# Transposes moved from TensorE to a DMA regrouping, and layer norms by sums, in a four-layer graph kernel

## The chip, the cores and the metric

The kernel runs on one core of one Trainium2 chip. The metric is the device time of one execution in microseconds (us), as a median of several executions. In what follows PE is TensorE, DVE is VectorE, ACT is ScalarE, POOL is GpSimd and SP is SyncE, the engine that issues the DMAs here.

## The reference, cut to what matters

Thirty-two graphs of 512 nodes with 256 channels pass through four attention layers, all over one mask `adj`. After each layer comes a residual addition and a layer norm without weights; layer 0 has two more layer norms inside it.

```python
x = _layernorm(x + _L0_gnn_ref(x, adj, w_qkv, ..., w1, b1, w2, b2))  # 8 heads, then a two-layer MLP
x = _layernorm(x + _L1_gnn_ref(x, W, a, adj))                        # additive scores, 1 head
x = _layernorm(x + _L2_gnn_ref(x, adj, W1, W2, W3))                  # product scores
x = _layernorm(x + _L3_gnn_ref(x, adj, W, a))                        # additive scores, 4 heads

def _layernorm(x, axis=-1, eps=1e-5):
    m = jnp.mean(x, axis=axis, keepdims=True)
    v = jnp.var(x, axis=axis, keepdims=True)
    return (x - m) / jnp.sqrt(v + eps)
```

Of the kernel before, what the change touches and what calls it, by code (L numbers as in the profile page):

```python
# [9 lines left out]
FP = mybir.dt.float32  # L10
# [20 lines left out]
AGE = 30.0  # L31
# [21 lines left out]
class Plan:  # L53
# [40 lines left out]
    def run(self, emit=True):  # L94
# [29 lines left out]
        while avail:  # L124
            cands = []
            for o in avail:
# [17 lines left out]
                for e, c in o.cost.items():  # L144
# [3 lines left out]
                    if best is None or key < best[0]:  # L148
# [5 lines left out]
                          key=lambda c: (not c[1].frees, c[1].graph * AGE - c[1].rank))  # L154
# [37 lines left out]
def kernel(  # L192
# [60 lines left out]
    def cbuf(shape, name, dt=FP):  # L253
# [37 lines left out]
        "D": [tc.dram_tile([H3, N], FP, name=f"r{i}") for i in range(6)],  # L291
        "PS": [psum.tile([P, N], FP, name=f"ps{i}") for i in range(8)],
# [5 lines left out]
    plan = Plan(slots, {"B": [14, 10, 10, 12], "S": [4] * 4, "T": [8] * 4, "D": [1] * 4, "PS": [0] * 4}, 5,  # L298
# [48 lines left out]
    def nodes(s):  # L347

        return lambda b: T2(b)[:, :, s * 2 * P:(s + 1) * 2 * P]

# [7 lines left out]

    def transposed(xs):

        xT = Buf("B")
        for s in range(2):
            ps = Buf("PS")

            def fn(e, s=s, ps=ps):
                for k in range(KC):
                    for j in range(2):
                        nc.tensor.transpose(two(ps)[:, k, j * P:(j + 1) * P],  # L368
                                            T4(xs)[:, 2 * s + j, k * P:(k + 1) * P], ident)
            op({"PE": 4 * TR}, fn, r=[xs[s]], w=[ps], pre=[xT])  # L370
            evac(ps, xT, s, nodes(s), two)
        return xT
# [12 lines left out]
    def project(xT, w, col, s, pre, row=None, part=None):  # L385

# [13 lines left out]
        op({"PE": 2 * F + (0.1 if row is None else 0.33)}, fn, r=[xT[part], w] + ([row] if row else []),  # L400
# [13 lines left out]
    def layernorm(y, dst, last=False, halves=(0, 1)):  # L414
        for s in halves:
            st, mv = Buf("T"), Buf("T")

            def stats(e, s=s, st=st, mv=mv):
                for j in range(2):
                    nc.vector.bn_stats(st.t[:, 6 * j:6 * j + 6], T4(y)[:, 2 * s + j, :])  # L420
                for j in range(2):
                    nc.vector.bn_aggr(mv.t[:, 2 * j:2 * j + 2], st.t[:, 6 * j:6 * j + 6])  # L422
            op({"DVE": 0.92}, stats, r=[y[s]], w=[st, mv])

            def scales(e, mv=mv):
                m = mv.t[:, :4].rearrange("p (c k) -> p k c", k=2)
                nc.gpsimd.tensor_scalar(mv.t[:, 4:6], m[:, 1, :], 1.0, EPS, ALU.mult, ALU.add)  # L427
                nc.gpsimd.tensor_tensor(mv.t[:, 6:8], mv.t[:, 4:6], mhalf[:, :2], ALU.pow)  # L428
                nc.gpsimd.tensor_scalar(mv.t[:, 8:10], m[:, 0, :], -1.0, 0.0, ALU.mult, ALU.add)
                nc.gpsimd.tensor_tensor(mv.t[:, 10:12], mv.t[:, 8:10], mv.t[:, 6:8], ALU.mult)  # L430
            op({"POOL": 1.6}, scales, r=[mv], w=[mv])
# [12 lines left out]
    def layer0(b, xs, xZ):  # L444
# [99 lines left out]
        u = Buf("B")  # L544
        for s in range(2):
            op(TH, lambda e, s=s: nc.vector.tensor_tensor(
                half(y, s), half(y, s), half(xs, s), ALU.add),
               r=[y[s], xs[s]], w=[y[s]])
        layernorm(y, u)
# [6 lines left out]
        hT, f, y2 = Buf("B"), Buf("B"), Buf("B")  # L556
        for k in range(KC):
            ps_h = project_t(w1_sb, 0, yT, k, hT)

            def relu(e, k=k, ps_h=ps_h):  # L560
                o, i, b = T2(hT)[:, k, :], ps_h.t, b1_sb.t[:, k:k + 1]
# [9 lines left out]
        for s in range(2):  # L571
            ps_f = project(hT, w2_sb, 0, s, f, c1p)
            op(TH, lambda e, s=s, ps_f=ps_f: nc.vector.tensor_tensor(
                half(f, s), ps_f.t, half(u, s), ALU.add), r=[ps_f, u[s]], w=[f[s]])
        layernorm(f, y2)
        for s in range(2):
# [3 lines left out]
            op(TH, lambda e, s=s: nc.vector.tensor_tensor(  # L580
                half(y2, s), half(y2, s), half(xs, s), ALU.add), r=[y2[s], xs[s]], w=[y2[s]])
        return y2

    def scored(xs, w, heads, val_shape, d1):
# [10 lines left out]

        xt = Buf("B")

        def xq():
            return xt.t[:, :NC * C].rearrange("p (q c b) -> p c q b", c=NC, b=32)
        for s in range(2):  # L600
            for c in (2 * s, 2 * s + 1):
                op({"DVE": cdve(256)}, lambda e, c=c: nc.vector.transpose(
                    xq()[:, c], T4(xs)[:, c, :].rearrange("p (q a) -> p q a", a=32)),
                    r=[xs[s]], w=[xt[s]])
# [51 lines left out]
    def layer1(xs):  # L656
# [7 lines left out]
        y, rinv = Buf("B"), Buf("T")  # L664
        for c in range(NC):
            ps = Buf("PS")

            def av(e, c=c, ps=ps):
# [7 lines left out]
            op({"DVE": 0.39}, lambda e, c=c, ps=ps: nc.vector.scalar_tensor_tensor(  # L676
                T4(y)[:, c, :], ps.t[:, :C], rinv.t[:, c:c + 1], T4(xs)[:, c, :],
                ALU.mult, ALU.add), r=[ps, rinv[c], xs[c // 2]], w=[y[c // 2]])
        track(NC * H0, NC, rinv, NC * H0)
        return y  # L680

    def layer2(xs):
        xT = transposed(xs)
        gT, v = Buf("B"), Buf("B")
        for k in range(KC):
            evac(project_t(w12_sb, 0, xT, k, gT), gT, k, lambda b, k=k: T2(b)[:, k, :])
# [3 lines left out]
        for s in range(2):  # L690
            evac(project(xT, w3_sb, 0, s, v, part=s), v, s, lambda b, s=s: vv()[:, 2 * s:2 * s + 2, :C], two)
        op({"DVE": 0.08}, lambda e: nc.vector.memset(vv()[:, :, C:C + 1], 1.0), r=[xT], w=[v])
        y = Buf("B")
        for s in range(2):
            a, low_, pT = Buf("B"), Buf("T"), Buf("B")
            for j in range(2):
# [46 lines left out]
            op(TH, lambda e, s=s: nc.vector.tensor_tensor(  # L743
                half(y, s), half(y, s), half(xs, s), ALU.add),
               r=[y[s], xs[s]], w=[y[s]])
        return y

    def layer3(xs):
# [45 lines left out]
        ex, y = Buf("B"), Buf("B")  # L794
# [665 lines left out]
```

## The kernel before: the parts that the change and the argument touch

The kernel doesn't issue its instructions graph by graph. It first describes each graph as operations, each with an estimated cost on each engine that could take it, and a list scheduler (the "plan") then simulates the engines and emits everything in one fixed order. On the chip each engine runs its own part of this order, strictly in order. So the scheduler's costs never run on the chip, but they decide what stands in front of what.

```python
AGE = 30.0
LAT = {"PE": 0.3, "DVE": 0.15, "ACT": 0.2, "POOL": 0.25, "SP": 4.0}   # from an operation's end to its result
# ... in Plan.run: an operation that can start first is placed; older graphs have priority
            s, o, e = min((c for c in cands if c[0] <= tmin + 0.05),
                          key=lambda c: (not c[1].frees, c[1].graph * AGE - c[1].rank))
# ...
            for n in o.succ:
                n.npred -= 1
                n.ready = max(n.ready, f + LAT[e])
# ... five graphs in flight:
    plan = Plan(slots, {"B": [14, 10, 10, 12], ...}, 5, {"DVE": 1.0})
    DMA = 0.53                                                        # planned cost of one DMA issue
```

Transposes for layer 0's MLP and for layer 2 are made on PE, eight of 128x128 for each, and copied out of PSUM by `evac`. A new graph comes in by `block`, four DMAs in runs of 128 bytes that leave each 32x32 block in a form that DVE can transpose:

```python
    def transposed(xs):
        xT = Buf("B")
        for s in range(2):
            ps = Buf("PS")
            def fn(e, s=s, ps=ps):
                for k in range(KC):
                    for j in range(2):
                        nc.tensor.transpose(two(ps)[:, k, j * P:(j + 1) * P],
                                            T4(xs)[:, 2 * s + j, k * P:(k + 1) * P], ident)
            op({"PE": 4 * TR}, fn, r=[xs[s]], w=[ps], pre=[xT])
            evac(ps, xT, s, nodes(s), two)
        return xT

    def layernorm(y, dst, last=False, halves=(0, 1)):
        for s in halves:
            # ... DVE: two bn_stats, two bn_aggr
            # ... POOL: four small instructions make scale and shift
            # ... ACT or DVE: two normalizations of 128x256

        def block(e, b=b, xZ=xZ):                       # the load of a new graph
            v = x[b].rearrange("(j b) (k i a) -> i b k j a", b=32, k=KC, i=4)
            for i in range(4):
                nc.sync.dma_start(
                    T2(xZ)[32 * i:32 * i + 32].rearrange("p k (j a) -> p k j a", a=32), v[i])
        op({"SP": 4 * DMA}, block, w=[xZ])
```

## Time and profile before

| | before |
|---|---|
| time, three executions | 3023.44 us (3019.7 to 3026.94) |
| span of the profiled execution | 3020.5 us |
| PE, DVE, ACT, POOL busy | 98%, 87%, 56%, 29% |
| PE lost in 2700 to 3021, by busy time | 53.9 us |

PE is busy in every microsecond from 200 to 2700. But a matmul that waits for its turn can count as busy, so I also kept a second account of PE, used below for every run. From the timeline of PE I took each group of equal instructions, from its start to the start of the next group, and subtracted the number of instructions times the shortest slot that such an instruction shows in a row (0.43 us for 512 columns of f32, about 0.216 for 256 columns, 0.109 for a transpose, and so on). What is left is lost. A loss of over 0.5 us at one place I call a gap; the rest, 0.1 to 0.3 at a time, are switches between matmuls of different shape. "Mid-run" is from 200 us to some 290 us before the end.

### The profile page before, as it was taken

The page shows a single profiled execution, that of the slowest core. Times are in us where ns is not written, and L with a number is a line of the kernel's source. Part 1 is how long each engine was busy: PE and PEld are TensorE (multiplying, and loading weights), DVE is VectorE, ACT ScalarE, POOL GpSimd, SP SyncE. Part 2 cuts the span into 40 slices and gives each one's busy share as a digit, 9 for nine tenths or more (in the row PEclk, how much of TensorE's full clock was granted, in tenths as well). Part 3 has the DMA queues.
Part 4 walks back from the last instruction along what each step waited for, and adds up shares of the span by engine and source line. Part 5 has one row for each costly group of instructions (what it writes and reads, how often), then busy time and mean ns, then how long its engine had stood idle before and what let it go on. Part 6 is the DMA issues. An engine that isn't in the chain of part 4 may idle for free.

```text
span 3020.5 us, 49063 instructions
## 1 busy us (share of the span) xinstructions
PE 2947.4 (98%) x17898; PEld 1633.3 (54%) x17898; DVE 2635.2 (87%) x5277; ACT 1688.5 (56%) x3475; POOL 866.8 (29%) x1809
## 2 busy tenths in 40 slices
PE   8999999999999999999999999999999999999885
PEld 3465555555555555555555555555555555555452
DVE  7988899988899988899988899988899988889754
ACT  5546655665655665555665555665555665655432
POOL 0223322322322322322322322322322322322221
PEclk9999999999999999999999999999999999999997
DMA  7000110111110110110110110110110111110000
GB/s 139 12 19 22 39 39 19 40 39 22 39 39 19 39 40 22 39 39 18 40 40 22 39 39 19 40 39 22 39 39 19 40 39 24 37 32 19 32 25 29
DMA packets 194746, 102.67 MB, mean 34 GB/s; under 512 B 143937, under 2 KB 181313, under 8 KB 194497
## 3 DMA queue, kind: packets, MB, share of 16 engines
q1 hardware_dynamic: 193648, 97.63, 12.9%
q8 instruction: 142, 2.33, 0.3%
q10 hardware_dynamic: 848, 1.84, 0.2%
q14 instruction: 108, 0.88, 0.1%
HBM read 82.31 MB, written 17.12 MB: 33 GB/s over the span
## 4 chain that ended last, share of the span: by engine, by line
PE 92%; DVE 4%; issue 1%; DMA 1%; ACT 1%; POOL 1%; SPq 1%; DVEq 0%; ACTq 0%; POOLq 0%
PE ps L380 15%; PE ps L397 11%; PE ps L467 9%; PE ps L475 8%; PE ps L611 8%; PE ps L765 7%; PE ps L730 7%; PE ps L703 7%; PE ps L670 7%; PE ps L771 4%; PE ps L368 2%; PE ps L722 2%; PE ps L536 1%; PE ps L701 1%; PE ps L802 1%
## 5 line engine op out<-in xcount | busy, mean ns | idle before, releaser
L340 ACT ACTIVATE b<-ps 128x512 f32<-128x512 f32 x772 | 434.9, 602 | 497.2 <-PE ps L380 186.9
L486 DVE TENSOR_TENSOR b<-b,maskT 128x1024 f32<-128x1024 f32 x512 | 594.5, 1212 | 25.1 <-ACT b L480 25.1
L480 ACT ACTIVATE b<-ps 128x512 f32<-128x512 f32 x1024 | 528.4, 604 | 116.7 <-PE ps L475 116.7
L439 ACT ACTIVATE b<-b,t 128x256 f32<-128x256 f32 x768 | 425.6, 597 | 255.9 <-POOL t L430 244.3
L427 POOL TENSOR_SCALAR t<-t 128x2 f32<-128x2 f32 x384 | 135.2, 352 | 845.0 <-DVE t L422 777.8
L757 DVE SCALAR_TENSOR_TENSOR b<-b,s,maskT 128x512 f32<-128x512 f32 x512 | 358.7, 740 | 8.0 <-DMA b<-r 7.7
L428 POOL TENSOR_TENSOR t<-t,mhalf 128x2 f32<-128x2 f32 x384 | 340.0, 885 | 32.0
L475 PE MATMUL ps<-b,b 32*128 32x512 f32 x2048 | 300.4, 640 | 0.0
L498 DVE TENSOR_TENSOR b<-b,b 128x1024 f32<-128x1024 f32 x256 | 297.4, 1210 | 0.0
L420 DVE BATCH_NORM_STATS2 t<-b 128x6 f32<-128x256 f32 x768 | 284.4, 412 | 7.8 <-DVE b L580 0.5
L408 POOL TENSOR_TENSOR acc<-acc,s 128x32 f32<-128x32 f32 (+2 forms) x96 | 77.3, 806 | 637.8 <-DVE s L525 378.1
L467 PE MATMUL ps<-b,b 128*32 128x512 f32 x2048 | 250.9, 598 | 2.6 <-DVE b L486 2.3
L765 PE MATMUL ps<-b,b 128*64 128x512 f32 x1024 | 239.3, 606 | 13.1 <-DVE b L757 13.1
L380 PE MATMUL ps<-b,wqkv_sb 128*128 128x512 f32 x512 | 248.1, 609 | 0.0
L397 PE MATMUL ps<-w_sb,b 128*128 128x256 f32 x1024 | 245.6, 388 | 1.4 <-ACT b L340 1.4
L703 PE MATMUL ps<-b,b 128*128 128x512 f32 x512 | 240.6, 592 | 0.0
L380 PE MATMUL ps<-b,w_sb 128*128 128x512 f32 x512 | 235.5, 603 | 2.5 <-ACT b L340 2.5
L670 PE MATMUL ps<-b,b 128*128 128x257 f32 x1024 | 230.8, 383 | 2.5 <-issue 2.5
L730 PE MATMUL ps<-b,b 128*128 128x257 f32 x1024 | 228.5, 380 | 0.4 <-ACT b L340 0.4
L670 PEld LDWEIGHTS ps<-b,b 128*128 128x128 f32 x1024 | 195.8, 192 | 45.4 <-issue 10.6
L397 PEld LDWEIGHTS ps<-w_sb,b 128*128 128x128 f32 x1024 | 190.0, 191 | 53.8 <-issue 30.0
L408 POOL TENSOR_TENSOR acc<-acc,t 128x2 f32<-128x2 f32 (+2 forms) x128 | 37.9, 308 | 598.7 <-DVE t L789 325.7
(124 smaller groups left out, 4129.8 us busy)
## 6 DMA issues: line engine op xcount, KB each, us to landing
b<-r SPq DMA_DIRECT2D x64, 512.0 KB
b<-in_x_dram SPq DMA_DIRECT2D x128, 128.0 KB
b<-in_x_dram SPq DMA_DIRECT2D x32, 512.0 KB
out_dram<-b SPq DMA_DIRECT2D x64, 256.0 KB
b<-r SPq DMA_DIRECT2D x32, 256.0 KB
r<-s SPq DMA_DIRECT2D x128, 0.5 KB
r<-s SPq DMA_DIRECT2D x128, 2.0 KB
b<-in_adj_dram ACTq DMA_DIRECT2D x4, 256.0 KB
```

The source lines that it names most:

```text
L340: nc.scalar.activation(dst, src, AF.Copy)
L380: nc.tensor.matmul(ps.t, w.t[:, i, col + k * P:col + (k + 1) * P], T2(xT)[:, i, :], start=(i == 0), stop=(i == KC - 1))
L397: nc.tensor.matmul(two(ps)[:, j, :], T2(xT)[:, i, c * P:(c + 1) * P], w.t[:, i, col:col + C], start=(i == 0 and row is None), stop=(i == K ...
L439: nc.scalar.activation(o, i, AF.Identity, bias=b, scale=sc)
L467: nc.tensor.matmul(ps.t[D0 * h:D0 * h + D0, :], lhs(h), T2(p[h // 2][c])[:, h % 2, :], start=start, stop=stop)
L475: nc.tensor.matmul(s[h].t, T2(kT)[r:r + D0, g, c * P:(c + 1) * P], T2(qT)[r:r + D0, g, :], start=True, stop=True)
L480: op({"ACT": cact(512)}, lambda e, c=c, j=j, i=i, s=s, p=p: nc.scalar.activation(T2(p[j][c])[:, i, :], s[2 * j + i].t, AF.Exp, scale=SC0), ...
L486: nc.vector.tensor_tensor(t, t, maskT[c].t.unsqueeze(1).to_broadcast([P, 2, N]), ALU.mult)
L670: nc.tensor.matmul(ps.t[:, :C + 1], T2(p[m // 2])[:, m % 2, c * P:(c + 1) * P], hv.t[:, m * (C + 1):(m + 1) * (C + 1)], start=(m == 0), st ...
L703: nc.tensor.matmul(ps.t, T2(gT)[:, i, c * P:(c + 1) * P], T2(xT)[:, i, :], start=False, stop=(i == KC - 1))
L730: nc.tensor.matmul(ps_o.t[:, :C + 1], T2(pT)[:, j, m * P:(m + 1) * P], vv()[:, m, :], start=(m == 0), stop=(m == NC - 1))
L765: nc.tensor.matmul(ps_o[h // 2].t[D3 * (h % 2):D3 * (h % 2 + 1), :], T4(hv)[:, m + i, h * D3:(h + 1) * D3], T2(p[i][h // 2])[:, h % 2, :], ...
```

## The change

The intent is to take work off the busiest engine, PE, and off the next one, DVE. It has three parts that can be told apart:

1. The **DMA regrouping**: DVE transposes 32x32 blocks in SBUF, one DMA writes the result (512 KB) to a buffer in DRAM, four DMAs read it back regrouped. No transposes on PE and no evacuations of them.
2. The **sums**: each residual addition also returns its row sums, and the squares are summed by ACT's activation with an accumulator, in place of bn_stats and bn_aggr on DVE.
3. The **plan**: six graphs in flight, age 15, and one common priority for the last four graphs.

```diff
-AGE = 30.0
+AGE = 15.0
+LAST = 4
-                          key=lambda c: (not c[1].frees, c[1].graph * AGE - c[1].rank))
+                          key=lambda c: (not c[1].frees, min(c[1].graph, len(self.graphs) - LAST) * AGE - c[1].rank))
-    plan = Plan(slots, {..., "D": [1] * 4, "PS": [0] * 4}, 5,
+    plan = Plan(slots, {..., "D": [1] * 4, "E": [1] * 4, "PS": [0] * 4}, 6,
     def transposed(xs):
-        ... (the PE transposes shown above)
+        xt, xT, d = quarters(xs), Buf("B"), Buf("E")
+        op({"SP": DMA}, lambda e: nc.sync.dma_start(d.t, xt.t[:, :NC * C]), r=[xt], w=[d])
+
+        def get(e):
+            v = d.t.rearrange("(j a) (k i n) -> i a k j n", a=32, i=4, n=P)
+            for i in range(4):
+                nc.sync.dma_start(T2(xT)[32 * i:32 * i + 32].rearrange(
+                    "a k (j n) -> a k j n", n=P), v[i])
+        op({"SP": 4 * DMA}, get, r=[d], w=[xT])
+    def add(y, s, a, b, sm, r):
+                nc.vector.tensor_tensor_reduce(
+                    T4(y)[:, 2 * s + j, :], a()[:, j], b()[:, j], 1.0, 0.0, ALU.add, ALU.add,
+                    sm[s].t[:, j:j + 1])
-                    nc.vector.bn_stats(...) / nc.vector.bn_aggr(...)
+                    nc.scalar.activation(T4(dst)[:, 2 * s + j, :], T4(y)[:, 2 * s + j, :], AF.Square,
+                                         bias=mv.t[:, j:j + 1], scale=-float(C),
+                                         accum_out=mv.t[:, 2 + j:3 + j])
+            op({"ACT": 2 * cact(C, 1) + 0.2}, squares, r=[y[s], mv[0]], w=[dst[s], mv[2]])
 ... (layers 0 to 3 return their sums along with y; views adapted to the regrouped order)
```

## The prediction

> **What bounds the kernel now.** I read the page first: busy shares, slices, chain of work.
>
> ```profile
> PE 2947.4 (98%) x17898; PEld 1633.3 (54%) x17898; DVE 2635.2 (87%) x5277; ACT 1688.5 (56%) x3475; POOL 866.8 (29%) x1809
> PE   8999999999999999999999999999999999999885
> PE 92%; DVE 4%; issue 1%; DMA 1%; ACT 1%; POOL 1%; SPq 1%; DVEq 0%; ACTq 0%; POOLq 0%
> ```
>
> TensorE (PE) is busy 98% of the span and carries 92% of the chain that ended last; only the first and the last three slices fall short. Busy alone proves little, since a waiting matmul can count as busy, so I checked stretches of the run next (columns: stretch, its length, busy time of PE, weight loads, VectorE (DVE), ScalarE (ACT), GpSimd, granted clock, DMA share, GB/s):
>
> ```profile
> 1000.00:2000.00 1000.00, 1000.00 (x6175) 554.24 (x6173) 902.69 (x1796) 579.58 (x1194) 301.80 (x609) 1.00 0.13 33
> 2800.00:2850.00 50.00, 39.15 (x286) 23.50 (x285) 40.11 (x82) 20.04 (x47) 13.17 (x27) 0.86 0.13 41
> 2900.00:2960.00 60.00, 51.97 (x281) 31.80 (x274) 29.35 (x75) 21.29 (x47) 8.37 (x26) 0.91 0.09 32
> 2960.00:3021.00 61.00, 26.01 (x155) 12.55 (x153) 24.42 (x60) 8.40 (x19) 5.73 (x20) 0.73 0.09 27
> ```
>
> In mid-run PE has no gap at all, VectorE is at 90% and not the bound. At the end PE loses 10.9 + 8.0 + 35.0 = 53.9 us. The chain in order of time around 1500 us (start, duration, what) shows real slots, from one piece to the next:
>
> ```profile
> 1513.47 1.02 PE ps L368 x8
> 1514.49 5.15 PE ps L380 x12
> 1519.65 0.44 PE ps L786 x4
> 1520.08 0.87 PE ps L802 x8
> ...
> 1577.32 1.91 PE ps L380 x4
> ```
>
> L368 is the transpose that the change removes. Four transposes cost 0.44 us and eight 0.87, so 0.109 each; eight cost 1.02 when they follow matmuls that use part of the array, and four projection records likewise 1.91 then and 1.72 (5.15 / 3) in a row. So a switch costs 0.15 to 0.20 us. From the groups of instructions:
>
> ```profile
> L368 PE MATMUL ps<-ident,b 128*128 128x128 f32 x512 | 71.8, 280 | 9.6 <-ACT b L439 9.5
> L420 DVE BATCH_NORM_STATS2 t<-b 128x6 f32<-128x256 f32 x768 | 284.4, 412 | 7.8 <-DVE b L580 0.5
> L422 DVE BATCH_NORM_AGGREGATE t<-t 128x2 f32<-128x6 f32 x768 | 114.9, 173 | 0.2
> L439 ACT ACTIVATE b<-b,t 128x256 f32<-128x256 f32 x768 | 425.6, 597 | 255.9 <-POOL t L430 244.3
> L937 DVE CUSTOM_DVE_ANT_0 b<-b,b 128x256 f32<-128x256 f32 x6 | 2.5, 425 | 2.4 <-DMA b<-in_L_gnn_a_dram 2.2
> L711 DVE DVE_READ_ACCUMULATOR2_ANT t<- 128x1 f32 x128 | 10.6, 83 | 0.0
> ```
>
> Dividing the busy time by the count gives a slot without overlap: 0.554 us for L439, not 0.597.
>
> **What the Trainium skill says.** "Trainium Kernel Development and Optimization", Performance Expectations, calls matmul busy time a bad metric since matmuls are pipelined. The trace agrees: L368 books 71.8 us, 512 x 0.109 is 55.8. "ScalarE: Activation LUTs", What ACT_TABLE_LOAD costs, gives 186 ns + 0.833 ns an element + about 93 ns for each pointer operand: 585 ns for 256 elements with two pointers, against 597 in L439. Its Table sets section says that cheap functions stand in every set; the trace has one table load in all, so I expect none for Square. "DMA: Bandwidth & Descriptors", Anatomy of one DMA, fits 2.0 us + bytes / 436e3 for another issuing path, 3.2 us for 512 KB; in this trace the broadcast load took 4.01 us near the end of the run. I use 4.
>
> **The change part by part.** TensorE: the 512 transposes go. Compared instruction by instruction in the built order, all other matmul counts are equal. Removed: 512 x 0.109 = 55.8 us. Switches from part-array matmuls to whole-array ones fall from 289 to 266 in the new order, and weighted by 0.15 to 0.19 that is 51 against 44 us, 7 less. Together 63; the chain gives L368 only 1.9% of the span, 57 us. I take 60.
>
> ScalarE: 128 evacuations of the transposes go (768 L340 copies of 512 become 640): 128 x 0.565 = 72 us. Of the normalizations 29 move to VectorE: 16 us. Added are 768 squares with an accumulator. Estimate from the skill page's formula: 186 + 93 + 213 = 492 ns, less 43 of overlap as in L439, plus 187 ns for an accumulator read (L845 shows one of 187): 0.64 us each, 489 us. Sum 1688 - 72 - 16 + 489 = 2090 us, 71% of the span.
>
> VectorE, removed: statistics 284.4 + 114.9; the four additions L546, L573, L580, L743 at 41.0 + 43.0 + 44.2 + 45.1; small transposes L602 97.8; L676 60.9; L815 43.4; total 774.7. Added: 512 summed additions of 256 at 0.417 (2.5 / 6 from L937) + 0.083 for the read = 256; 256 transposes of 512 at 0.656 (L449, 42.0 / 64) = 168; L676's successor 128 x (0.476 + 0.083) = 72; L815's 128 x (0.417 + 0.083) = 64; 29 normalizations, 9. Total 569. VectorE falls by some 206 us to 2430, 82%.
>
> GpSimd keeps four instructions per half layer norm. DMA: 64 writes of 512 KB and 256 reads of 128 KB in 512-byte runs, 67 MB on top of 103; the mean share of 0.13 may become 0.2. A round trip is about 4 + four issues of 0.6 + 4 = 10 to 11 us, where the transpose and its copies took some 2 or 3; a sixth graph in flight fills that, as the existing round trip through DRAM is filled (L757 waited for it 7.7 us in the whole run, once). All 39 big buffers are as before.
>
> So in mid-run PE stays the bound with more slack beneath it, and the 60 us count in full. As a check: two graphs between the same points of the score matmuls come to 185.7 us of PE slots before and 182 after, 2.0%. Over the same stretch VectorE's demand runs ahead of PE's by 39 us at the worst before and 25 after.
>
> **Ends.** The last four graphs now share one priority, so they end together. From the last layer-0 score matmul in the built order, 199 us of PE slots remain, against 152 of VectorE and about 140 of ScalarE: PE stays the bound there. But the last PE instructions are transposes of all four graphs in a row, and after them everything drains at once. VectorE does 8 x 0.644 and 8 x 0.642 first, then the first pair of sums (1.0), then ScalarE 16 squares (10.2) and 15 normalizations (8.3): 29.8 us, starting some 3 before PE ends, then 4 to 6 for the store and the end: about 31. Before, the drain was 15.5 us, from 3005 in these lines to 3020.5:
>
> ```profile
> 3004.40 0.56 PE ps L802 x3
> 3004.98 1.29 DVE b L805 x2
> ...
> 3014.33 0.14 DVE bad L1037
> ```
>
> With 8 us of gaps earlier in the tail I get 39 lost instead of 53.9, so 15 gained. In the first 200 us PE loses 20 before; VectorE has less to do at first, so I take 4 off. Sum: 3020.5 - 60 - 15 - 4 = 2941.5 of span, plus 3 (3023.4 is the time, 3020.5 the span), near 2945.
>
> **Rivals.** (a) ScalarE becomes the pacing engine where layer norms bunch up: each now goes VectorE, ScalarE, GpSimd, ScalarE, in order, and the same queue evacuates PSUM. For it: its work grows by 24%, and before it already waited 244 us for GpSimd's L430. Against: 71%, and in built order its demand never runs more than 5 us ahead of PE's. It would give 20 to 40 us back: 2965 to 2985. (b) The round trip is not hidden, as one in-order queue issues everything and a store waiting for its data holds up the rest (SyncE's wait for L439 sums to 1222 us, the longest 47.7). 64 trips exposed by 1 us each give back 64 us and leave "same", about 3005. Against: those waits are mostly an empty queue. (c) The end gains more than I think, since work of four graphs fills the gaps: 2920. (d) Square needs a table switch each time: far slower; against it the skill page, so 1%.
>
> **Range and chances.** Parts: TensorE 55 to 63, ends 5 to 35, given back 0 to 40. That puts 80% at 2915 to 2983. Two per cent is 2963: only when much is given back do I miss it. Faster 0.74, same 0.25, slower 0.01.
>
> **What would show it.** Right: no L368-like transposes, PE still 100% in mid-run stretches, VectorE near 2430, ScalarE near 2090, PE busy near 2885, a drain after the last PE group of 25 to 35 us. Wrong: PE waits on DMA for the regrouped buffer or on ScalarE's squares in mid-run, or more than one table load. Squares much above 0.64 us apiece, or PE gaps of over 1% in mid-run, would break the prediction.

## More of the kernel before

The issue queue of SP in mid-run of the kernel before (start, duration, line, transfer, count): two stores of a finished graph, then the four DMAs of a new graph's block load, L994.

```profile
1438.57 2.47 SPq L1013 DMA_DIRECT2D out_dram<-b  x2
1441.50 2.77 SPq L994 DMA_DIRECT2D b<-in_x_dram  x4
```

The four issues take 2.8 us and DVE begins the transposes of the new graph at 1449.06, 7.6 us after the first issue. As DVE waits for this load only three times in the whole run, 7.6 us is an upper bound of its landing.

Line numbers shift by the change. After it, L386 is a projection (L380 before), L467 the block transposes of a new graph (L449 before), L493 the score matmuls of layer 0, L402 another projection, L738 the attention product of layer 2, L763 the masking of scores in layer 3, L440 the squares, L423 the summed additions, L1004 the block load (L994 before), L370 and L375 the regrouping's write and reads, L657 the broadcasts of layer 3's scores, and L1023 the stores.

## The result, and the profile after

The changed kernel took 2995.02 us (2993.75 to 2996.51, four executions), the kernel before 3022.16 in the same rounds. The ratio is 0.9908 (95% interval 0.9891 to 0.9926): within 2%, "same". Ratios here are the mean time of one kernel's fast runs over that of the other's of the same rounds, so not quite the ratio of the medians. The prediction, 2945 with a range of 2915 to 2983, was wrong: 27 of the 78 us foretold came.

The page of the changed kernel, busy shares, PE slices, and the chain of work that ended last:

```profile
PE 2899.6 (97%) x17385; PEld 1579.0 (53%) x17386; DVE 2409.6 (80%) x4858; ACT 1958.7 (65%) x4854; POOL 776.0 (26%) x1809
PE   8999999999999999999999999999999999999995
PE 61%; ACT 12%; DVE 8%; SPq 5%; DMA 3%; POOL 3%; issue 2%; DVEq 0%; ACTq 0%
```

The slices look as good as before, better at the end. The chain doesn't: PE carries 61% of it instead of 92%, and SP's issue queue rises from 1% to 5%, DMA from 1% to 3%. Of the views, the chain alone says at once that something new paces the kernel. The stretches confirm it (columns as in the prediction):

```profile
1000.00:2000.00 1000.00, 979.60 (x5866) 532.16 (x5858) 815.58 (x1633) 660.09 (x1646) 254.02 (x605) 1.00 0.21 56
2900.00:2994.00 94.00, 61.48 (x416) 27.51 (x414) 61.77 (x143) 35.82 (x93) 20.69 (x53) 0.85 0.10 36
```

In mid-run PE now has 20 us without any work in 1000 us, where it had none. My account of PE's slots finds more, as part of each wait is booked as busy:

| us | before | after | difference |
|---|---|---|---|
| slots (work) | 2842.1 | 2786.0 | -56.1 |
| lost 0 to 200 | 41.3 | 37.1 | -4.2 |
| mid-run, switches | 48.7 | 45.8 | -2.9 |
| mid-run, gaps over 0.5 us | 0 | 78.0 | +78.0 |
| lost in the last 290 | 72.4 | 28.0 | -44.4 |
| before the first and after the last group | 16.0 | 18.4 | +2.4 |
| sum (the span) | 3020.5 | 2993.3 (span 2993.5) | -27.2 |

So the transposes did go in full, and the end got better by more than I thought; 78 us came back in mid-run, as gaps (that this is as much as the whole gain foretold is chance). Of them 41.2 lie between L738 and the first projection of a new graph, L386 (the first kind below); 27.5 between the start of a group of scores, L493, and L402 (the second kind: 1.25 us in each of 22 graphs); 9 elsewhere. The waits of engines (us in total, times, longest), first of the kernel after:

```profile
DVE b L467 <- DMA b<-in_x_dram: 70.2, 27, 3.1
PE ps L386 <- DVE b L467: 33.8, 24, 2.1
```

and of the kernel before:

```profile
DVE b L449 <- DMA b<-in_x_dram: 9.4, 3, 6.4
```

DVE waits for the block load of a new graph in 27 of 32 graphs, where it did so three times, and PE then waits for DVE. One case in the timeline of the kernel after, SP's issue queue, then DVE, then PE (start, duration; in brackets the idle time before and what ended it):

```profile
1583.62 0.35 SPq L370 DMA_DIRECT2D e<-b  x1
1584.20 1.06 SPq L657 DMA_DIRECT2D b<-r  x2
1585.39 0.90 SPq L1023 DMA_DIRECT2D out_dram<-b  x2
1586.33 7.81 SPq L1004 DMA_DIRECT2D b<-in_x_dram  x4
1594.19 2.66 SPq L375 DMA_DIRECT2D b<-e  x4
```

```profile
1596.70 1.30 DVE L467 STREAM_TRANSPOSE b<-b 128x512 f32<-128x512 f32 x2 [2.53 <-DMA b<-in_x_dram]
```

```profile
1588.65 7.12 PE L738 MATMUL ps<-b,b 128*128 128x257 f32 x32
1597.47 4.99 PE L386 MATMUL ps<-b,wqkv_sb 128*128 128x512 f32 x11 [1.70 <-DVE b L467]
```

Within 2.7 us SP issues the regrouping's write (512 KB), two broadcasts (512 KB each) and two stores (256 KB each), 2 MB, and right behind them the block load. Its four issues, 2.8 us before, now take 7.8 us, and the data is there 10.4 us after the first issue. The order has DVE's transposes of that graph, and PE's projections after them, placed for the 6.1 us of the plan (4 x 0.53 + 4.0, after the issue of the first DMA). DVE stands still for 2.5 us in front of L467, PE for 1.7. Over all graphs the issue of the four has a median of 6.8 us (before: 2.9), and from first issue to DVE's start 10.35 us pass (before: 7.9, mostly without a wait).

The delay then travels. The chain that ended last, around 1500 us, in order of time:

```profile
1500.71 4.05 DMA b<-in_x_dram
...
1505.58 0.67 DVE b L467
...
1508.36 4.63 DVE b L763 x7
...
1515.53 0.98 ACT b L440 x4
1516.51 0.49 ACT b L498
...
1517.04 1.12 PE ps L493 x2
```

The late DVE catches up on its masking (L763), ACT gets its squares (L440) late, the exponentials (L498) that free PSUM for the scores stand behind them, and PE waits a second time, before the last two of the eight scores of that group (L493 x2): the second kind of gap, which the account books in front of L402.

The groups of the new instructions, to check the prices of the prediction (busy, mean ns of one, idle before):

```profile
L440 ACT ACTIVATE b<-b,t 128x256 f32<-128x256 f32 x768 | 382.1, 502 | 193.9 <-DVE t L423 172.2 <-DVE b L682 12.9 <-DVE b L825 7.8
L440 ACT ACTIVATION_READ_ACCUMULATOR b<-b,t 128x1 f32 x768 | 148.1, 193 | 0.0
L423 DVE CUSTOM_DVE_ANT_0 b<-b,b 128x256 f32<-128x256 f32 x384 | 144.0, 420 | 3.5 <-ACT b L747 2.1
```

The accumulator read of 193 ns is mostly covered by the square after it. The timeline of ACT shows a pair (two squares and two reads) from start to next start:

```profile
1572.55 0.50 ACT L440 ACTIVATE b<-b,t 128x256 f32<-128x256 f32 x1
...
1573.53 0.57 ACT L715 ACTIVATE b<-ps 128x512 f32<-128x512 f32 x1
```

1573.53 - 1572.55 = 0.98 us for a pair, 0.49 for one, not 0.64.

### The profile page after: what moved, and what is told of

Read it like the earlier page. It is cut to its first block, busy times and chain, and to the rows that moved or that the text cites. A ratio compares the mean times of both kernels' runs of the same rounds, so it can differ in the third digit from the quotient of the medians.

```text
span 2993.5 us, 49482 instructions
## 1 busy us (share of the span) xinstructions
PE 2899.6 (97%) x17385; PEld 1579.0 (53%) x17386; DVE 2409.6 (80%) x4858; ACT 1958.7 (65%) x4854; POOL 776.0 (26%) x1809
## 4 chain that ended last, share of the span: by engine, by line
PE 61%; ACT 12%; DVE 8%; SPq 5%; DMA 3%; POOL 3%; issue 2%; DVEq 0%; ACTq 0%
PE ps L386 9%; PE ps L485 9%; PE ps L771 8%; PE ps L493 7%; PE ps L402 7%; PE ps L617 6%; ACT b L440 5%; DVE b L763 5%; SPq L1004 5%; PE ps L777 4%; DMA b<-in_x_dram 3%; PE ps L711 3%; PE ps L676 3%; ACT b L457 3%; PE ps L738 2%
## 5 line engine op out<-in xcount | busy, mean ns | idle before, releaser
L498 ACT ACTIVATE b<-ps 128x512 f32<-128x512 f32 x1024 | 530.7, 626 | 115.2 <-PE ps L493 114.3
L342 ACT ACTIVATE b<-ps 128x512 f32<-128x512 f32 (+1 forms) x644 | 364.8, 601 | 247.5 <-PE ps L777 151.7
L440 ACT ACTIVATE b<-b,t 128x256 f32<-128x256 f32 x768 | 382.1, 502 | 193.9 <-DVE t L423 172.2
L457 ACT ACTIVATE b<-b,t 128x256 f32<-128x256 f32 x739 | 406.3, 607 | 130.5 <-POOL t L448 130.1
L763 DVE SCALAR_TENSOR_TENSOR b<-b,s,maskT 128x512 f32<-128x512 f32 x512 | 350.4, 744 | 46.2 <-DMA b<-r 46.2
L493 PE MATMUL ps<-b,b 32*128 32x512 f32 x2048 | 323.7, 641 | 3.5 <-ACT b L498 0.3
L447 POOL TENSOR_TENSOR t<-t,mhalf 128x2 f32<-128x2 f32 x384 | 313.4, 816 | 32.0
L413 POOL TENSOR_TENSOR acc<-acc,s 128x4 f32<-128x4 f32 (+2 forms) x96 | 37.0, 385 | 903.0 <-ACT s L622 827.4
L386 PE MATMUL ps<-b,wqkv_sb 128*128 128x512 f32 x512 | 233.9, 608 | 36.9 <-DVE b L467 33.8
L485 PE MATMUL ps<-b,b 128*32 128x512 f32 x2048 | 251.1, 603 | 0.2
L386 PE MATMUL ps<-b,w_sb 128*128 128x512 f32 x512 | 244.8, 607 | 0.0
L402 PE MATMUL ps<-w_sb,b 128*128 128x256 f32 x1024 | 244.2, 386 | 0.0
L738 PE MATMUL ps<-b,b 128*128 128x257 f32 x1024 | 231.1, 382 | 3.9 <-ACT b L342 3.9
L771 PE MATMUL ps<-b,b 128*64 128x512 f32 x1024 | 233.8, 598 | 0.0
L361 DVE STREAM_TRANSPOSE b<-b 128x512 f32<-128x512 f32 x256 | 177.2, 700 | 55.9 <-ACT b L457 55.2
L402 PEld LDWEIGHTS ps<-w_sb,b 128*128 128x128 f32 x1024 | 188.8, 190 | 44.0 <-issue 16.5
```

The costliest lines, as they stand in the source:

```text
L342: nc.scalar.activation(dst, src, AF.Copy)
L386: nc.tensor.matmul(ps.t, w.t[:, i, col + k * P:col + (k + 1) * P], T2(xT)[:, i, :], start=(i == 0), stop=(i == KC - 1))
L402: nc.tensor.matmul(two(ps)[:, j, :], T2(xT)[:, i, c * P:(c + 1) * P], w.t[:, i, col:col + C], start=(i == 0 and row is None), stop=(i == K ...
L440: nc.scalar.activation(T4(dst)[:, 2 * s + j, :], T4(y)[:, 2 * s + j, :], AF.Square, bias=mv.t[:, j:j + 1], scale=-float(C), accum_out=mv.t ...
L457: nc.scalar.activation(o, i, AF.Identity, bias=b, scale=sc)
L485: nc.tensor.matmul(ps.t[D0 * h:D0 * h + D0, :], lhs(h), T2(p[h // 2][c])[:, h % 2, :], start=start, stop=stop)
```

## The experiments

Two theories stood after the traces. **A**: a new graph's block load lands later than the plan assumes, as it is issued behind the traffic of the regrouping and the stores; the gaps of the first kind follow from it. **B**: ScalarE is late, because the plan prices a pair of squares too low or because there is simply more for it to do in front of the exponentials; the gaps are ACT's. The expectations also name **C**, that the added DMA traffic slows the queue whatever the order, and **D**, that the new order puts 2 MB in front of the load on one queue. Another matter was how much of the gain at the end belongs to the plan alone. Sixteen kernels ran. Changing a cost or a constant of the plan changes the whole order of instructions, and the account below (in us, as above) shows how much else moves then; only four experiments (shortsq, xwide, xone, both) keep the order of the changed kernel exactly, at the price of a wrong result.

| run | median | ratio (95%) | gaps in mid-run | lost in the last 290 |
|---|---|---|---|---|
| before | 3022.2 | | 0 | 72.4 |
| after | 2995.0 | 0.9908 (0.9891 to 0.9926) | 78.0 | 28.0 |
| xlat | 3062.5 | 1.0127 (1.0108 to 1.0146) | 119.3 | |
| sqcost | 2935.8 | 0.9716 (0.9700 to 0.9733) | 9.8 | 49.0 |
| last0 | 3010.7 | 0.9958 (0.9941 to 0.9974) | 85.5 | 36.8 |
| oldplan | 2992.9 | 0.9894 (0.9878 to 0.9911) | 1.4 | 77.7 |
| shortsq | 2974.5 | 0.9842 (0.9826 to 0.9858) | 49.8 | |
| planonly | 3004.0 | 0.9939 (0.9922 to 0.9956) | 3.5 | 48.6 |
| nodma | 2987.6 | 0.9885 (0.9869 to 0.9902) | 3.4 | 38.9 |
| nosums | 3013.7 | 0.9961 (0.9943 to 0.9978) | 70.8 | 65.5 |
| xact | 3207.4 | 1.0605 (1.0587 to 1.0622) | 258.5 | |
| xwide | 2954.8 | 0.9771 (0.9755 to 0.9787) | 40.3 | |
| age14 | 3440.7 | 1.1379 (1.1356 to 1.1401) | 532.5 | |
| age14sq | 2923.2 | 0.9667 (0.9648 to 0.9687) | 7.2 | 27.3 |
| xone | 2950.4 | 0.9756 (0.9740 to 0.9772) | 36.2 | |
| lat16 | 2944.1 | 0.9745 (0.9729 to 0.9762) | 6.4 | 39.6 |
| lat155 | 2916.6 | 0.9650 (0.9634 to 0.9666) | 0.6 | 34.4 |
| both | 2933.0 | 0.9705 (0.9689 to 0.9721) | 8.2 | |

The kernel before lay between 3021.7 and 3024.0 in the rounds of these. Where a cell is empty, the loss was not worked out. The edits below are against the changed kernel unless said otherwise.

### xlat: the plan is told that the block load lands 8 us later

```diff
-    def op(self, cost, fn, r=(), w=(), pre=()):
+    def op(self, cost, fn, r=(), w=(), pre=(), lat=0.0):
-                n.ready = max(n.ready, f + LAT[e])
+                n.ready = max(n.ready, f + LAT[e] + o.lat)
-        op({"SP": 4 * DMA}, block, w=[xZ])
+        op({"SP": 4 * DMA}, block, w=[xZ], lat=8.0)
```

> Changed kernel, but the planner is told that the load of a new graph's x block lands 8 us later than it assumed, so the order on every engine puts that graph's first transposes and projections later; no work changes. Theory A (the 41 us that TensorE loses between the second attention product of layer 2 and a new graph's projections come from the order expecting that load too early): these gaps fall under 10 us in mid-run, time 2955 to 2965. Theory B (ScalarE is late, since the order takes two squares for 1.0 us where they take 1.4, and everything behind it is late): the gaps move to other places, time 2985 to 3000. Theory C (the added DMA traffic itself slows the queue, whatever the order): gaps at the same place, shorter at most by a third, 2980 to 2995.

It was slower, 3062.5 us, outside all three forecasts, and the gaps grew to 119.3 us. Its waits of PE (total, times, longest) name another transfer:

```profile
PE ps L386 <- DMA b<-e: 43.4, 10, 10.0
```

PE now waited for the regrouped buffer. A as I had put it to the test, that a later landing time in the plan would close the gaps, fell here. With 8 us the plan was wrong in the other direction by about as much (14.1 us, where 10.4 were measured in the changed kernel), and the new order made different collisions. A cost in the plan is a blunt tool for a test, as everything behind it moves too.

### sqcost: a pair of squares is planned at 1.4 us instead of 1.0

```diff
-            op({"ACT": 2 * cact(C, 1) + 0.2}, squares, r=[y[s], mv[0]], w=[dst[s], mv[2]])
+            op({"ACT": 2 * cact(C, 1) + 0.6}, squares, r=[y[s], mv[0]], w=[dst[s], mv[2]])
```

> Changed kernel, but the planner takes a pair of squares for 1.4 us on ScalarE instead of 1.0; no work changes. Theory B: ScalarE comes to be on time, both kinds of mid-run gaps shrink (41 us before a new graph's projections, 27 us of short waits for a PSUM bank before value projections), time 2930 to 2955. Theory A: only the 27 us go, time 2965 to 2980. Theory C: under 15 us gained, 2980 or more.

2935.8 us, 3% under the kernel before, with gaps of 9.8 us instead of 78: by the expectation, B's outcome. It is no proof of B. A pair takes 0.98 us on the chip, so the price of 1.0 was right and 1.4 is wrong. SP's queue in this kernel shows what else happened:

```profile
1452.20 3.16 SPq L1004 DMA_DIRECT2D b<-in_x_dram  x4
1455.40 1.17 SPq L657 DMA_DIRECT2D b<-r  x2
```

In the order that came out, the block load stands in front of the two broadcasts, its issue takes 3.2 us (median) and it is there after 6.9 us. So the order changed what A speaks of, too, and the run agrees with A as well as with B.

### last0: the last four graphs have their own priorities again

```diff
-LAST = 4
+LAST = 0
```

> Changed kernel without the rule that the last four graphs share one priority. If that rule is what took the 44 us off TensorE's losses after 2700 us, the time rises by 25 to 45 us, to 3020 to 3040, and mid-run is untouched. If the gain at the end came from the operations (less VectorE work), it stays within 10 us of 2995.

15.7 us slower than the changed kernel: 8.8 more lost at the end, 7.5 more in gaps. It lies between the two forecasts. With the common priority of the last graphs goes a gain of 16 us, half of it at the end.

### oldplan: the new operations with the old plan (age 30, five graphs, no common priority)

```diff
-AGE = 15.0
-LAST = 4
+AGE = 30.0
+LAST = 0
-    plan = Plan(slots, {...}, 6,
+    plan = Plan(slots, {...}, 5,
```

> The new operations with the old plan: five graphs in flight, age weight 30, no rule for the last graphs. Theory A: a new graph's projections stand late enough again, as in the kernel before, mid-run gaps over 0.5 us under 15 us in all, end as long as in the kernel before (72 us lost): 2960 to 2985. Theory B: the waits for ScalarE stay, 2985 to 3015. A rival to both: with five graphs the DRAM round trips are no longer hidden, and TensorE waits for the regrouped buffer: over 3010.

2992.9 us. Gaps in mid-run are gone (1.4 us), as A foretold, with the same transfers, which speaks against C; the four issues take 3.0 us here (median). But 77.7 us are lost at the end and the switches in mid-run come to some 70 us, so that the time missed A's 2960 to 2985. So neither the regrouping nor the squares make gaps by themselves: they do in the new order. The old order has no gap and no gain at the end; the new one has both.

### shortsq: squares over 16 elements (wrong), same order

```diff
-                    nc.scalar.activation(T4(dst)[:, 2 * s + j, :], T4(y)[:, 2 * s + j, :], AF.Square,
+                    nc.scalar.activation(T4(dst)[:, 2 * s + j, :16], T4(y)[:, 2 * s + j, :16], AF.Square,
-                nc.gpsimd.tensor_scalar(mv.t[:, 4:6], mv.t[:, 2:4], float(C) ** -3, EPS, ALU.mult, ALU.add)
+                nc.gpsimd.tensor_scalar(mv.t[:, 4:6], mv.t[:, 2:4], 16.0 * float(C) ** -3, EPS, ALU.mult, ALU.add)
```

> Wrong result on purpose: the changed kernel in exactly its own order of instructions on every engine, but each square runs over 16 elements instead of 256 (the sum is scaled up by 16), so that a pair takes about 1.0 us on ScalarE, as the planner believed, instead of 1.4. Theory B (ScalarE runs late against the order because squares are longer than planned): TensorE's mid-run gaps over 0.5 us fall from 78 us to under 20, time 2925 to 2950. Rival (the run with the larger planned cost was fast because it drew a luckier order, not because ScalarE was on time): gaps stay over 60 us, time over 2980.

2974.5 us, 20.6 under the changed kernel and between the two forecasts. ACT's work fell from 1959 to 1827 us. A pair takes 0.65 us now; the 1.4 us of the expectation was a misreading, as a pair took 0.98 before. The gaps in front of the new graph's projection stayed (41.2 to 43.5 us). Those of the second kind shrank. One such group of scores, first in the changed kernel, then here:

```profile
1424.11 2.40 PE L493 MATMUL ps<-b,b 32*128 32x512 f32 x8
```

```profile
1414.87 1.64 PE L493 MATMUL ps<-b,b 32*128 32x512 f32 x8
```

A group without a wait takes 1.14 us. In each of 22 graphs a loss of 1.25 us became one of 0.50. As that is just the limit of the account, the account has 2.5 us of gaps left there and 28.2 fewer in all, which is too much: 27.5 us fell to 11, and the time by 20.6. So ScalarE has a part in the second kind of gap and none in the first, the larger one. B is no explanation of the whole.

### planonly: the operations of before with the new plan

```diff
(against the kernel before)
-AGE = 30.0
+AGE = 15.0
+LAST = 4
-                          key=lambda c: (not c[1].frees, c[1].graph * AGE - c[1].rank))
+                          key=lambda c: (not c[1].frees, min(c[1].graph, len(self.graphs) - LAST) * AGE - c[1].rank))
-    plan = Plan(slots, {...}, 5,
+    plan = Plan(slots, {...}, 6,
```

> The operations of the kernel before with the new plan alone (six graphs in flight, age weight 15, one priority for the last four). Theory B: no squares, so nothing is planned too short: mid-run as dense as before, the end some 40 us shorter, 2965 to 2990. Rival (the new plan itself, by putting new graphs' projections early, makes the gaps): mid-run gaps of 40 us or more, 3000 or more.

3004.0 us, 18 under before: 24 gained at the end (72.4 to 48.6), where 40 were expected, and some 9 lost in mid-run, 3.5 of them in gaps, so the plan makes hardly any by itself. It brings two thirds of what the whole change brought.

### nodma: sums and new plan, transposes left on PE

```diff
     def transposed(xs):
-        xt, xT, d = quarters(xs), Buf("B"), Buf("E")
-        ... (write and four reads)
+        ... (PE transposes and evacuations of before, with their views)
```

> The changed kernel with the transposes back on TensorE and ScalarE (no regrouping through DRAM), sums and squares and the new plan kept. Theory B: the gaps stay (60 us or more in mid-run), so 3020 to 3060. Theory C (the added DMA traffic and the full queue are the cause): gaps gone, 2965 to 2995.

2987.6 us, faster than the changed kernel although PE has its 56 us of transposes. Gaps are 3.4 us with the squares in place: C's forecast came, B's (60 us or more) did not. With oldplan this says that the gaps need both, the transfers and an order that puts them in a bad place. Under this plan, taking 56 us off PE made the kernel 7 us slower.

### nosums: regrouping and new plan, layer norms by bn_stats

```diff
(against the kernel before: AGE, LAST, six graphs and transposed() of the change; layernorm() kept)
```

> The changed kernel with the old layer norm (statistics on VectorE, no squares on ScalarE), regrouped transposes and the new plan kept. Theory B: mid-run gaps under 20 us, time 2925 to 2950. Theory C: gaps of 40 us or more stay, 2965 or more. A third outcome: VectorE, with 400 us of statistics back and 70 us more of transposes, becomes the bound: over 2990 with VectorE at 90% or more in mid-run.

3013.7 us. The busy line of the page:

```profile
PE 2903.4 (96%) x17386; PEld 1600.3 (53%) x17386; DVE 2685.3 (89%) x5277; ACT 1623.7 (54%) x3347; POOL 763.3 (25%) x1809
```

The regrouping puts block transposes on DVE, which without the sums is at 89% (92% from 1000 to 2000 us): the third outcome of the expectation, and a rival for these gaps. They are 70.8 us, at other places than in the changed kernel (L477 to L485 23.1, L390 to L613 17.4, lines of its own kernel). This run can't decide between A and B, since its order is another and the squares don't exist in it. It does show that gaps can come along with the regrouping even without squares on ACT. With planonly, nodma and the changed kernel it makes a square: under this plan the sums save 16 to 19 us and the regrouping costs 7 to 10. But each of the four kernels has an order of its own, so these are differences of kernels, not prices of the parts.

### xact: the block load is issued from ScalarE's queue

```diff
-                nc.sync.dma_start(
+                nc.scalar.dma_start(
                     T2(xZ)[32 * i:32 * i + 32].rearrange("p k (j a) -> p k j a", a=32), v[i])
```

> The changed kernel in its own order, except that the four block loads of a new graph are issued from ScalarE's DMA queue instead of SyncE's, at the same point of the plan. Theory D (the load stands behind 2 MB of transfers that the new order puts in front of it on one queue: the write for regrouping, two broadcasts, two stores; issuing it therefore takes 6.8 us instead of 2.9, and it lands late): the gaps before a new graph's projections fall from 41 to under 15 us, time 2955 to 2975. Rival (the 16 DMA engines themselves are full then, whichever queue feeds them): ScalarE is held by the issue for 5 us or more a graph, gaps as large or larger, 2990 or more. Rival A (the projections are simply too early): gaps of 30 us or more stay.

It was 6% slower than before. ACT's timeline and PE's waits:

```profile
1512.77 8.27 ACTq L1004 DMA_DIRECT2D b<-in_x_dram  x3
```

```profile
PE ps L738 <- ACT b L342: 182.0, 24, 8.5
```

The issue is as stretched on another engine's queue (8.7 us in the median), and the last three of the four hold ScalarE for 8.3 us, during which ACT evacuates no PSUM. This is the rival's outcome in the expectation. So it isn't SP's queue that is slow: SP and ACT were both held when they issued these transfers at that point. What holds it inside the DMA system no view here shows; that the same four issues take 2.9 us when only two stores stand in front of them (the kernel before) is measured.

### xwide: the block load in rows of 4 KB, four transfers as before (wrong), same order

```diff
-            v = x[b].rearrange("(j b) (k i a) -> i b k j a", b=32, k=KC, i=4)
+            v = x[b].rearrange("(i b c) d -> i b c d", b=32, i=4)
                 nc.sync.dma_start(
-                    T2(xZ)[32 * i:32 * i + 32].rearrange("p k (j a) -> p k j a", a=32), v[i])
+                    xZ.t[32 * i:32 * i + 32, :NC * C].rearrange("p (c d) -> p c d", c=NC), v[i])
```

> Wrong result on purpose: exactly the changed kernel's order, but the block load moves the same 512 KB in rows of 4 KB instead of 128-byte runs, 32 times fewer pieces. If the queue is held by the number of pieces of this load (Theory D in the form: the queue's room for pieces is used up), issue takes under 3 us and the gaps of 41 us fall under 10: 2950 to 2970. If it is the bytes in front of it, landing stays late: gaps over 30 us, 2985 to 2998.

This is the direct test of A: same order, same bytes, same traffic in front, only quicker to issue (2.7 us) and to land (8.7 us instead of 10.35). 2954.8 us, as foretold for a queue held by the number of pieces; the gaps in front of the new graph's projection fell from 41.2 to 7.7 us, those in front of L402 stayed (26.1). Total gaps went down by 37.7 us, 1.45 for each of 26 graphs in mid-run, where the load was 1.62 us earlier. So the lateness of the load makes the first kind of gap. The run also says something of the stretched issue: behind the same traffic, with rows of 4 KB in place of 128 bytes, it is gone. It takes both, the large transfers in front and the short runs of the load.

### age14 and age14sq: age 14, with the squares at 1.0 and at 1.4

```diff
-AGE = 15.0
+AGE = 14.0
(age14sq also has the edit of sqcost)
```

> The changed kernel with age weight 14 instead of 15, an arbitrary nudge that gives another order. If the order is not a matter of luck, 2980 to 3005; if small nudges alone move the time by as much as the planned cost of squares did (60 us), below 2960 or above 3020.

> The same nudge with a pair of squares planned at 1.4 us. If the planned cost itself is what helps, 2925 to 2955, at least 25 us below the run with age weight 14 and squares at 1.0. If the earlier 60 us were luck of the order, within 15 us of that run.

age14 took 3440.7 us, 15% more than the changed kernel, from one unit of a scheduling constant; its chain shows layer 3 of the oldest graph exposed, step by step, through its round trip in DRAM, and its gaps lie at quite other places (L493 to L709 153 us, L402 to L771 150, within L771 107). age14sq took 2923.2 (there the issues take 3.3 us and the load is there after 7.2, medians). Neither speaks for A or B: they show that orders found by this scheduler differ by far more than the effects that I was testing. From here on I trusted only runs with the same order, or an account of gaps.

### xone: the block load as one transfer of 128 rows of 4 KB (wrong), same order

```diff
-            v = x[b].rearrange("(j b) (k i a) -> i b k j a", b=32, k=KC, i=4)
-            for i in range(4):
-                nc.sync.dma_start(
-                    T2(xZ)[32 * i:32 * i + 32].rearrange("p k (j a) -> p k j a", a=32), v[i])
+            nc.sync.dma_start(xZ.t[:, :NC * C], x[b].rearrange("(p c) d -> p (c d)", p=P))
```

> Wrong result on purpose: the changed kernel's own order, but the block load of a new graph is one transfer of 128 rows of 4 KB instead of four of short runs, so that it should take some 5 us from first issue to landing instead of 10.2 in the changed kernel and 8.6 in the run with rows of 4 KB in four transfers. Loop theory (mid-run is paced by one loop, from the load through VectorE's transposes, ScalarE's squares, TensorE and the last layer norm to the next load, which is 2.9 us a graph longer than TensorE's work; whatever shortens it takes away either gap): both kinds of gaps vanish, under 12 us in mid-run, 2915 to 2935. Theory of two separate causes (the late load makes the gap before the projections, a late ScalarE makes the one before value projections): 25 us or more of the second kind stay, as in the run with 4 KB rows, 2938 to 2958.

2950.4 us. Issue 0.93 us, landing 8.28 us after it, 2.07 earlier than in the changed kernel; gaps 41.8 us fewer, 1.61 a graph. DVE's wait for the load fell from 70.2 to 20.6 us. The second kind fell too, from 27.5 to 19.9 us. Against xwide that is 4 us more, and the first kind has no part in it. Of the forecasts neither came: the time is that of two separate causes, but less than 25 us of the second kind stayed.

The trace shows why. Take the lead that DVE has over PE in a graph, from the start of its transposes L467 to PE's first projection L386. In the changed kernel the lead is 0.8 us in all 22 graphs that lose the 1.25 us: PE stands right behind the late DVE. In xone it varies, and the second loss with it (23 graphs of mid-run; the first and the last two are left out, as the order differs there):

| lead of DVE, us | 0.8 | 1.0 | 1.2 to 1.3 | 1.4 to 1.5 | 1.9 to 2.1 | 2.4 to 2.5 |
|---|---|---|---|---|---|---|
| second loss of a graph, us | 1.25 | 1.1 to 1.2 | 0.8 to 0.9 | 0.6 to 0.7 | 0.1 to 0.2 | 0 |
| graphs | 8 | 3 | 5 | 3 | 2 | 2 |

Each 0.1 us of lead takes 0.1 us off the loss. So an earlier load first closes the first gap; what it brings beyond that becomes lead, which closes the second. The second kind hangs on the late load, too.

### lat16 and lat155: the plan is told the measured landing time

Both have the edit of xlat, with 4.5 us in place of 8. The plan then takes the load to be there after 6.1 + 4.5 = 10.6 us; 10.35 was measured. The squares stay at their right price.

```diff
-AGE = 15.0
+AGE = 16.0        (lat16; lat155: 15.5, and LAST = 2)
-        op({"SP": 4 * DMA}, block, w=[xZ])
+        op({"SP": 4 * DMA}, block, w=[xZ], lat=4.5)
```

> Correct kernel: the planner is told that the block load lands 4.5 us later than it assumed (as the trace measures), squares at their original planned cost of 1.0 us for a pair (which the trace confirms: two squares and their accumulator reads take 0.98 us from start to start), age weight 16. If the error that mattered was the load's landing, TensorE is dense in mid-run (gaps under 15 us) without any change to the squares' cost: 2910 to 2945. If the planned cost of squares was what mattered: gaps of 40 us or more, over 2960.

> Correct kernel, as the one before with age weight 15.5 and the last two graphs sharing a priority instead of four: a candidate to beat both kernels. Dense in mid-run, a drain shorter than with four graphs ending together (31 us): 2900 to 2930. If the order is still fragile: anywhere up to 2990.

lat16 took 2944.1 us with 6.4 us of gaps, lat155 2916.6 with 0.6, both as foretold, and DVE waits for the block load in no graph. The result of both is right, and lat155 beats both kernels: 3.5% under before, 78 us under the changed one. A stretch of lat155 and its issue queue:

```profile
1000.00:2000.00 1000.00, 1000.00 (x6088) 556.48 (x6087) 842.77 (x1694) 701.50 (x1714) 294.14 (x625) 1.00 0.21 59
```

```profile
1440.56 2.84 SPq L1005 DMA_DIRECT2D b<-in_x_dram  x4
1443.57 1.06 SPq L658 DMA_DIRECT2D b<-r  x2
```

PE is dense again with ACT at 70% in mid-run, more than in the changed kernel, so ScalarE is not what limits it. And the loads go out in front of the large transfers; their four issues have a median of 3.0 us. A reservation is due: two or three constants differ from the changed kernel at once, and after age14 I would not claim that the landing time alone did it.

### both: xwide and shortsq together (wrong), same order

```diff
(the edits of xwide and of shortsq)
```

> Wrong result on purpose: the changed kernel's own order with both edits, block loads in rows of 4 KB and squares over 16 elements. One alone took 38 us and the other 28 us off the 78 us of mid-run gaps. If the late load and ScalarE's squares together carry the loss, the effects add: 8 to 20 us of gaps left, 2920 to 2935. If they hid one another or a third cause stands behind: over 30 us of gaps left, over 2940.

2933.0 us with 8.2 us of gaps, as foretold. In the account shortsq took 28.2 us of gaps away, xwide 37.7, and both 69.8, but the losses of 0.50 us at its limit are here again, so I compare times. shortsq is 20.6 us faster than the changed kernel, xwide 40.2, and both together 62: they add up (60.8). So some 62 us of the 78 are accounted for; of the rest about 11 us are the short waits that stay in the second kind. That xwide left that kind as it was (27.5 to 26.1) fits xone's table: its 1.62 us went into the first gap, and in most graphs the lead stayed at 0.8 us.

## Why the prediction was wrong, point by point

- **The work on PE** was right: "512 x 0.109 = 55.8" against 56.1 in the account, and the switches fell by 2.9 us where 7 were expected: 59.0 for the 60 us taken. PE's busy time is 2899.6 for "near 2885", because some waits book as busy.
- **The step that failed** is "So in mid-run PE stays the bound with more slack beneath it, and the 60 us count in full." PE's work did shrink by this, but it had 78.0 us of gaps in mid-run, where there had been none. Rival (b) came nearest: its in-order queue, its 64 us and its "about 3005" are close to 78 and 2995, but at another place. It had looked at the regrouped buffer, and PE waited for that once in the changed kernel, for 0.8 us. What stood behind the new traffic was the load of the next graph. My argument against (b), that SP's waits are mostly an empty queue, was about the average of the run; 2 MB within 2.7 us right in front of the block load is a matter of one place, and could have been read from the built order of SP.
- **What is shown and what isn't.** Shown, at unchanged order: an earlier load makes the kernel 40 to 45 us faster (xwide, xone), shorter squares 21 (shortsq), the load of xwide and shorter squares together 62. So the late load is the larger cause. Two things make the second kind together: the late load, carried on through DVE (xone's table), and ScalarE's squares in front of the exponentials (shortsq). Rival (a), ScalarE pacing, held in this small part although ACT is busy only 65% of the span. Shown also: the gaps belong to the order, as oldplan with the same operations has 1.4 us of them. Left open: why the orders of sqcost and age14sq are so good, beyond a load that is earlier than in the changed kernel; and what stretches the issue inside the DMA system.
- **VectorE** was right: 2409.6 us against 2430. **ScalarE** was over-priced: 1958.7 against 2090. The mis-sized term is the square, "0.64 us each": I added the whole accumulator read, but it overlaps, and one takes 0.49. 768 x 0.15 = 115 of the 131 us too much. The single table load was right. The chip had more room on ACT than I thought, and PE waited for it all the same.
- **The ends.** Lost by busy time after 2700 us, the measure that the prediction used: 53.9 before, 294 - 260.8 = 33.2 after, where I predicted 39: 21 gained instead of 15. By slots it is more, 42 us with the last bit, because before the change waits near the end were booked as busy. The gain needs the plan: planonly has 24 us of it with the old operations, oldplan none of it with the new ones. The head gained 4.2 us, as "I take 4 off" said.
- **The drain** was 37.5 us, from 2956 to 2993.5, against "about 31". The chain there goes through other work than I had put in it:

```profile
2954.05 1.90 PE ps L777 x16
...
2969.50 0.30 POOL t L434
...
2984.22 0.20 PE ps L1040 x2
```

  After VectorE's part it is GpSimd's small instructions of eight half layer norms that follow one another from 2969.5 to 2983.6, 14 us, not ScalarE's squares and normalizations.
- **The sum.** Predicted 3020.5 - 60 - 15 - 4 = 2941.5. Measured 3020.5 - 59.0 - 42.0 - 4.2 + 78.0 = 2993.3. Had "given back 0 to 40" held, the kernel would have been within the range. With a plan that avoids the collision the kernel does get there and beyond (lat155), so the regrouping can be worth having (lat155 without it was not run); under the plan that it came with, the kernel without it was 7 us faster (nodma).

## What to carry to other kernels

Before crediting work taken off a busy engine, look where the transfers that replace it stand in the issuing queue, and what stands right behind them: the victim here was an innocent load, and the share of busy time and the mean DMA share (0.21) hid it. Where an order is planned from estimated costs, measure each estimate in the trace, landing times above all, after every change of traffic. And test a cause with the order of instructions held fixed: a change of one constant of the plan moved the time by 15%, over five times the effect in question.

## What the Trainium skill lacked or had wrong

- "DMA: Bandwidth & Descriptors", Issuing engines are not separate DMA queues, says that issuing from several engines only saves the time to initiate a DMA, "which is usually small relative to the DMA itself". Its first half agrees: moved to ScalarE, the same load was as slow (8.3 us for three of the four issues). The second half doesn't hold here: four issues took 6.8 us (median) of the 10.35 until the data was used, and 2.9 us with only two stores in front. Nor did I find a figure in the skill for how long an engine is held in its issue by transfers issued before.
- "ScalarE: Activation LUTs", What ACT_TABLE_LOAD costs: its formula gives an estimate of 492 ns for a square with one pointer, 502 measured, and of 585 for a normalization with two, 607 measured. It has no word on the accumulator read, a separate instruction of 193 ns of which most overlaps: a square with its read takes 0.49 us in a row.
- None of the pages that I read has the cost of a VectorE instruction that adds and sums 128x256 in one pass: 420 ns.
